# Feed-forward rows as two float32r parts, with the scale on VectorE

## The chip, the cores and the metric

The kernel runs on one core of a Trainium2 chip. The engines of the core are TensorE (PE, matmuls; its weight loads are shown apart as PEld), VectorE (DVE), ScalarE (ACT), GpSimd (POOL) and SyncE (SP, which issues most DMAs). Each works through its own queue in order, and they wait for each other through semaphores. The metric is the device time of one execution in microseconds (us).

## The reference

Four sequences of 2048 tokens with 512 features go through one layer: attention with 16 heads of 32 features, a residual and a layer norm, then a feed-forward layer whose weights are only the signs of the given matrix, a residual and a layer norm again.

```python
q, k, v = (heads(x @ W.T) for W in (Wq, Wk, Wv))
attn = softmax(einsum('nhqd,nhkd->nhqk', q, k) / sqrt(32), axis=3)
x = layernorm(x + einsum('nhql,nhld->nhqd', attn, v))      # heads joined to 512
w = (weights >= 0) * 2 - 1                                  # plain signs, 512 x 512
y = clip(einsum('bsi,oi->bso', x, w) * scale + bias, -100, 100)
x = layernorm(x + y)
```

`scale` and `bias` have one value for each of the 512 outputs. Everything is float32.

## The kernel before

The work is cut into 16 units `n`: four batches of four head groups, each of four heads. A unit has four query blocks `qb` of 512 queries, and a query block has 16 steps, one for each 128 keys. So there are 64 steps in a unit and 1024 in all. The text below calls 16 steps a block and 64 steps a group.

A step does the following, whatever else it carries. `scores` puts the negated row maximum (a bf16 matmul, line 300) and the products of keys and queries (line 306) into four PSUM banks, one for each head, and ScalarE takes the exponentials into a tile `p` (line 313; four buffers of it). `max_unit` computes the scores of a later step a first time (line 248) and VectorE reduces three of the four banks to row maxima (line 255); the fourth is first copied to `moved` by ScalarE (line 267). Every second step, `weighted` multiplies two tiles `p` with the values (line 324), and VectorE adds the result to `oT` (line 336). `add_up` lets POOL add the tiles `p` of a block into `acc` (line 344), for the softmax denominators: 14 additions a block, one for each step but the first and the last.

The other work is spread over the steps as small pieces by a planner (`plan`). Pieces of kind "small" are transpositions, pieces of kind "big" are the projections to K, Q and V (line 206) and the feed-forward (`ffn`, line 532), at most two of the big ones in an odd step, chosen by due time and by a quota for each group. The planner also keeps a rough clock of PE, ACT and DVE (`runs`, `spend`, `give`), by which `take` picks the PSUM bank out of eight that should be free first. The program's order on each engine is fixed when it is built.

The part around the change is the class `Finish`, for one block of 512 tokens whose attention is complete: `load`, `stats`, `rstd` (its power runs on POOL, line 490), `shift` and `norm` make the first layer norm; `turn` transposes a row tile of 128 tokens into PSUM (line 518) and ScalarE copies it to SBUF (line 524); `ffn` multiplies it with the transposed signs `wT["ws"]` (line 532), and VectorE adds the bias (line 537), clips (line 538) and adds the residual (line 540); then comes the second layer norm and the store. For batches 0 to 2 this happens during the steps of the next batch, one row tile per 13 or 11 steps. For the last batch, `finish_last` and `finish_end` squeeze it into the last steps and behind them. The feed-forward of a row tile is cut by columns into thirds of 172, 172 and 168, each a big piece of its own; the last eight row tiles are done whole. There are 64 row tiles in all. The transposed rows lie in `nT` (two buffers), or, for the last batch, in `room`, a larger tile with place for four rows that `make_room` takes from another pool.

The signs are prepared once at the start by POOL (`sign_weights`, lines 147 and 149): the sign and the scale of each output row go into the weight matrix, before it is transposed.

Of the kernel before, what the change touches and what calls it, by code (L numbers as in the profile page):

```python
# [10 lines left out]

F32 = mybir.dt.float32
BF16 = mybir.dt.bfloat16
AF = mybir.ActivationFunctionType
ALU = mybir.AluOpType
AX = mybir.AxisListType
# [4 lines left out]
def kernel(  # L21
# [13 lines left out]
    P = 128  # L35
# [11 lines left out]
    MAX_VAL = 100.0  # L47
    SM_SCALE = 1.0 / math.sqrt(HD)
    STEPS = NQB * NT
    THIRDS = (0, 172, 344, D)  # L50
    W = 2 * P
    LEAD = NT + 6

# [78 lines left out]

    def transpose_weight(name, ic):
        if ic == 0:
            wT[name] = const.tile([P, DC, D], F32, name=f"{name}T")
        i = take()
        pt = cols_of(i, DC, P)
        for oc in range(DC):
            nc.tensor.transpose(pt[:, oc, :], raws[name][:, oc, ts(ic, P)], ident)  # L139
        runs("full", 0.44)  # L140
        nc.scalar.copy(wT[name][:, ic, :].rearrange("p (c o) -> p c o", c=DC), pt)
        give(i, "ACT", 0.6)

    def sign_weights():

        ws = raws["ws"]
        nc.gpsimd.tensor_scalar(ws, ws, 0.0, 2.0, ALU.is_ge, ALU.mult)
        for oc in range(DC):
            nc.gpsimd.tensor_scalar(
                ws[:, oc, :], ws[:, oc, :], 1.0, scale_t[:, oc : oc + 1], ALU.subtract, ALU.mult  # L150
            )

    raws = {n: load_weight(w, n) for n, w in (("wk", wk), ("wq", wq))}
    scale_t = const.tile([P, DC], F32, name="scale_t")
    bias_bc = const.tile([P, D], F32, name="bias_bc")

    def load_rest():
        for n, w in (("wv", wv), ("ws", w_ffn)):
            raws[n] = load_weight(w, n)
        nc.sync.dma_start(out=scale_t, in_=ffn_scale.rearrange("(c p) -> p c", p=P))  # L160
        nc.sync.dma_start(out=bias_bc, in_=ffn_bias.partition_broadcast(P))


# [283 lines left out]
    class Finish:  # L447
# [66 lines left out]
        def turn(self, j):  # L514
            i = take()
            pt = cols_of(i, DC, P)
            for c in range(DC):
                nc.tensor.transpose(pt[:, c, :], self.row(j)[:, ts(c, P)], ident)  # L518
            runs("full", 0.44)
            if self.b < B - 1:  # L520
                self.nT[j] = work.tile([P, DC, P], F32, tag="nT", name="nT")
            else:
                self.nT[j] = self.room[:, j, :].rearrange("p (c q) -> p c q", c=DC)
            nc.scalar.copy(self.nT[j], pt)
            give(i, "ACT", 0.6)

        def ffn(self, j, third):
            cols = slice(0, D) if third is None else slice(THIRDS[third], THIRDS[third + 1])
            i = take()
            py = ps[:, i, : cols.stop - cols.start]  # L530
            for c in range(DC):
                nc.tensor.matmul(  # L532
                    py, lhsT=self.nT[j][:, c, :], rhs=wT["ws"][:, c, cols],
                    start=(c == 0), stop=(c == DC - 1),
                )
            runs("full", 6.8e-3 * (cols.stop - cols.start))
            nc.vector.tensor_tensor(py, py, bias_bc[:, cols], ALU.add)
# [5 lines left out]
        def make_room(self):  # L543

            if self.g < NQB // 2:
                t = kpool.tile([P, S], F32, tag="kT", name="room") if self.g == 0 else shared[0]
                shared[:] = [t]
                self.room = t.rearrange("p (j d) -> p j d", j=NTQ)
            else:
                self.room = xpool.tile([P, NTQ, D], F32, tag="xg", name="room")  # L550

        def store_tile(self, j):
            nc.sync.dma_start(
# [27 lines left out]
    def finish(b, qb, a, every, w, lag):  # L581
        f = Finish(b, qb)
        at(a, f.load)
        for j in range(NTQ):
            at(a + 2 + j, f.stats, 1, j)
        at(a + 6, f.rstd, 1)
        at(a + 7 + lag, f.shift, 1)
        for j in range(NTQ):
            t = a + 8 + lag + every * j
            at(t, f.norm, 1, j)  # L590
            turned = task("small", t + 1, t + 3, f.turn, j)
            for k in range(3):
                task("big", t + 2, t + w, f.ffn, j, k, after=turned)
            at(t + w, f.stats, 2, j)
        e = a + 9 + lag + every * (NTQ - 1) + w
        at(e, f.rstd, 2)
        at(e + 1 + lag, f.shift, 2)
        for j in range(NTQ):
            at(e + 2 + lag + j, f.norm, 2, j)
        at(e + 5 + lag, f.store)  # L600

    def finish_last(qb, last):

        f = Finish(B - 1, qb)
        at(last - 9, f.load_last)
        a = last + 7
        late = qb == NQB - 2
        at(a + 1, f.make_room)
        for j in range(NTQ):
            at(a + j // 2, f.stats, 1, j)  # L610
        at(a + 2, f.rstd, 1)
        at(a + 4, f.shift, 1)
        for j in range(NTQ):
            t = a + 5 + (j if late else 3 * j)
            by = t + 6
            at(t, f.norm, 1, j)
            if late:
                by = total + (-1, 1, 4, 5)[j]
            turned = task("small", t + 1, t + 3, f.turn, j)
            for k in [None] if late else range(3):  # L620
                task("big", by if late else t + 2, by, f.ffn, j, k, after=turned)
            at(by + late, f.stats, 2, j)
        e = total + 7 if late else a + 21
        at(e, f.rstd, 2)
        at(e + 2, f.shift, 2)
        for j in range(NTQ):
            at(e + 3 + j, f.norm, 2, j)
        at(e + 7, f.store)

    def finish_end(qb, last):  # L630

        f = Finish(B - 1, qb)
# [8 lines left out]
        at(total + 3, f.make_room)  # L641
# [223 lines left out]
```

## Time and profile before

| what | value |
|---|---|
| time, median of 3 runs | 4386.38 us (4384.66 to 4386.73) |
| the profiled execution | 4386.25 us |
| its span, first to last instruction | 4384.5 us |
| granted TensorE clock, mean | 0.998 |
| exponentials, ACT, 128x512 | 4096 of 602 ns |
| additions of `p`, POOL, 128x2048 | 889 of about 4.54 us |
| feed-forward matmul lines, PE | 172 or 168 columns, 1344 records (two to a product); 512 columns, 64 records |
| copy of a turned row, ACT | 48 of 641 ns (`nT`), 16 of 608 ns (`room`) |
| bias, clip, residual, DVE | 172 columns: 337, 346, 332 ns; 512 columns: 696, 700, 687 ns |

In the groups of instructions, "mean ns of one" is the time from an instruction's start to its end; matmuls overlap in PE's pipeline, so the spacing of their starts tells more. Idle time is put down to what ended it. The chain of waits follows the last instruction back to what released each step. A table of stretches gives the busy time of each engine between two times, and the timeline shows merged runs of instructions with their start, length and number.

### The profile page before, as it was taken

To read this page: it belongs to the slowest core of one execution; us is meant where nothing else is said; L and a number is where in the kernel's file an instruction comes from. 1 tells how busy PE (TensorE), PEld (TensorE's weight loads), DVE (VectorE), ACT (ScalarE), POOL (GpSimd) and SP (SyncE) were. 2 spreads that over 40 slices of the span, in tenths; PEclk is the share of its full clock that TensorE was granted. 3 is DMA by queue.
4 is the path that set the end of the run, shared out by engine and by line. 5 is a ranking of instruction groups with operands and counts; after the bars stand their busy time and mean duration, and the time that the engine had idled before them with its cause. 6 is when DMAs were issued, how large, how long until landed. Compare 5 with 4: busy or idle time off the path is not lost.

```text
span 4384.5 us, 89302 instructions
## 1 busy us (share of the span) xinstructions
PE 4345.0 (99%) x36092; PEld 2135.5 (49%) x36092; DVE 3315.9 (76%) x5908; ACT 2999.3 (68%) x6173; POOL 4083.3 (93%) x940
## 2 busy tenths in 40 slices
PE   9999999999999999999999999999999999999998
PEld 5444444444454454455445454455544545455443
DVE  6777777777777777777777777777777777777774
ACT  4666666676667667676676766767667676767665
POOL 3999999999999999999999999999999999999993
PEclk9999999999999999999999999999999999999999
DMA  2000000010001000011000100001100000001101
GB/s 88 11 10 14 11 14 10 12 39 22 21 13 27 13 23 20 11 45 36 21 20 11 33 10 21 23 10 49 25 20 21 20 21 23 20 11 33 24 23 49
DMA packets 263351, 101.41 MB, mean 23 GB/s; under 512 B 169372, under 2 KB 239004, under 8 KB 262936
## 3 DMA queue, kind: packets, MB, share of 16 engines
q1 hardware_dynamic: 257656, 91.50, 8.6%
q8 instruction: 282, 4.62, 0.4%
q10 hardware_dynamic: 5280, 4.19, 0.3%
q14 instruction: 133, 1.09, 0.1%
HBM read 54.26 MB, written 33.02 MB: 20 GB/s over the span
## 4 chain that ended last, share of the span: by engine, by line
PE 91%; POOL 6%; DVE 1%; ACT 1%; issue 1%; DMA 0%; ACTq 0%; POOLq 0%; DVEq 0%
PE ps L324 20%; PE ps L248 19%; PE ps L306 19%; PE ps L206 15%; PE ps L300 8%; POOL acc L344 6%; PE ps L532 5%; PE ps L350 3%; PE ps L391 1%; PE ps L195 1%; PE ps L518 1%; ACT p L313 1%; DVE part L255 1%; DMA xs<-in_L_attn_x_dram 0%; PE ps L139 0%
## 5 line engine op out<-in xcount | busy, mean ns | idle before, releaser
L344 POOL TENSOR_TENSOR acc<-acc,p 128x2048 f32<-128x2048 f32 x825 | 3743.7, 4538 | 102.8 <-ACT p L313 42.6
L313 ACT ACTIVATE p<-ps 128x512 f32<-128x512 f32 x4096 | 2114.8, 602 | 1136.0 <-PE ps L306 1108.2
L255 DVE TENSOR_REDUCE part<-ps 128x1 f32<-128x512 f32 x3072 | 1933.0, 683 | 774.6 <-PE ps L248 774.2
L248 PE MATMUL ps<-kT,qT 32*128 32x512 f32 x8192 | 1114.3, 590 | 0.2 <-DVE xg_last L434 0.2
L306 PE MATMUL ps<-qT,kT 32*128 32x512 f32 x8192 | 1073.3, 591 | 0.0
L324 PE MATMUL ps<-p,vv 128*32 128x512 f32 x8192 | 983.4, 598 | 1.8 <-ACT p L313 1.8
L248 PEld LDWEIGHTS ps<-kT,qT 32*128 32x128 f32 x8192 | 542.8, 184 | 381.0 <-issue 194.5
L255 DVE TENSOR_REDUCE part<-moved 128x1 f32<-128x512 f32 x1024 | 691.9, 676 | 3.3 <-ACT moved L267 3.2
L267 ACT COPY moved<-ps 128x512 f32<-128x512 f32 x1024 | 631.0, 616 | 22.1 <-PE ps L248 18.0
L324 PEld LDWEIGHTS ps<-p,vv 128*32 128x32 f32 x8192 | 220.2, 109 | 686.9 <-issue 345.9
L300 PE MATMUL ps<-negm,ones_bf 32*128 32x512 bf16 x4096 | 443.1, 384 | 4.9 <-ACT p L313 2.9
L306 PEld LDWEIGHTS ps<-qT,kT 32*128 32x128 f32 x8192 | 405.8, 184 | 44.3 <-issue 27.5
L336 DVE TENSOR_TENSOR oT<-ps,oT 128x512 f32<-128x512 f32 x448 | 309.7, 691 | 97.4 <-PE ps L324 59.2
L344 POOL TENSOR_TENSOR acc<-p 128x2048 f32<-128x2048 f32 x64 | 290.8, 4544 | 96.0 <-ACT p L313 95.8
L300 PEld LDWEIGHTS <-ones_bf 32*128 32x128 bf16 x4096 | 105.6, 91 | 551.0 <-issue 522.3
L206 PEld LDWEIGHTS ps<-wvT,xT 128*128 128x128 f32 x2048 | 250.9, 191 | 80.3 <-ACT p L313 75.6
L206 PE MATMUL ps<-wvT,xT 128*128 128x128 f32 x2048 | 279.2, 280 | 0.3 <-ACT p L313 0.2
L206 PE MATMUL ps<-xT,wqT 128*128 128x256 f32 x1024 | 248.8, 386 | 2.7 <-ACT p L313 2.7
L206 PE MATMUL ps<-xT,wkT 128*128 128x256 f32 x1024 | 248.7, 387 | 0.0
L206 PEld LDWEIGHTS ps<-xT,wkT 128*128 128x128 f32 x1024 | 184.9, 190 | 68.8 <-ACT p L313 47.0
L206 PEld LDWEIGHTS ps<-xT,wqT 128*128 128x128 f32 x1024 | 184.5, 190 | 66.6 <-ACT p L313 44.9
L532 PEld LDWEIGHTS ps<-wsT,nT 128*128 128x128 f32 x1152 | 167.8, 189 | 94.2 <-ACT p L313 93.3
(75 smaller groups left out, 1722.4 us busy)
## 6 DMA issues: line engine op xcount, KB each, us to landing
xs<-in_L_attn_x_dram SPq DMA_DIRECT2D x64, 256.0 KB
xc<-in_L_attn_x_dram SPq DMA_DIRECT2D x60, 256.0 KB
res<-xc SPq DMA_DIRECT2D x60, 256.0 KB
xg<-res SPq DMA_DIRECT2D x12, 1024.0 KB
out_dram<-xg SPq DMA_DIRECT2D x12, 1024.0 KB
xg_last<-res SPq DMA_DIRECT2D x4, 768.0 KB
out_dram<-xg_last SPq DMA_DIRECT2D x3, 1024.0 KB
raw_wk<-in_L_attn_Wk_dram ACTq DMA_DIRECT2D x4, 256.0 KB
```

What stands on the lines that cost most here:

```text
L206: nc.tensor.matmul(pp, lhsT=lhs(c), rhs=rhs(c), start=(c == 0), stop=(c == DC - 1))
L248: nc.tensor.matmul(ps[:, banks[h], :], lhsT=qT[n, qb][rows, ts(qc, P)], rhs=kT[n][rows, ts(kb, QB)], start=True, stop=True,)
L255: nc.vector.tensor_reduce(part[:, qc, h : h + 1, kb], src, AX.X, ALU.max, negate=True)
L267: nc.scalar.copy(moved, ps[:, banks[-1], :])
L300: nc.tensor.matmul(ps[:, banks[h], :], lhsT=ones_bf[rows, :], rhs=negm[n, qb][rows, :], start=True, stop=False,)
L306: nc.tensor.matmul(ps[:, banks[h], :], lhsT=kT[n][rows, ts(kc, P)], rhs=qT[n, qb][rows, :], start=False, stop=True,)
L313: nc.scalar.activation(p[:, h, :], ps[:, banks[h], :], AF.Exp, scale=SM_SCALE)
L324: nc.tensor.matmul(pb[cols, :], lhsT=vv[n][:, kc, cols], rhs=p[:, h, :], start=(i == 0), stop=(i == 1),)
L336: nc.vector.tensor_tensor(outs[n, qb], pb, outs[n, qb], ALU.add)
L344: nc.gpsimd.tensor_tensor(a, before if kc == 1 else a, p, ALU.add)
L350: nc.tensor.matmul(ps[h * HD : (h + 1) * HD, b, :], lhsT=ones, rhs=p[:, h, :], start=start, stop=stop,)
L532: nc.tensor.matmul(py, lhsT=self.nT[j][:, c, :], rhs=wT["ws"][:, c, cols], start=(c == 0), stop=(c == DC - 1),)
```

## The change

Five things change together.

- `turn` makes two parts of a transposed row tile in place of one copy. ScalarE writes `high` as float32r, which keeps twelve significant bits, and VectorE subtracts it from the row in PSUM and writes the rest as `low`, float32r too. Both have two buffers, for all batches; `room` and `make_room` are gone.
- The transposed signs are a float32r tile, plain -1 and 1. POOL no longer multiplies the scale into them: its second operation is one instruction over all columns in place of four.
- `ffn` multiplies both parts with the signs, eight products into one bank in place of four.
- The scale is loaded as a row of 512 copied to all partitions (`scale_bc`), and VectorE multiplies each result by it, ahead of the bias.
- A row tile's feed-forward is cut into two halves of 256 columns in place of three thirds. The last eight row tiles are still done whole. The planner's clock gets new numbers for the pieces.

```diff
     def transpose_weight(name, ic):
         if ic == 0:
-            wT[name] = const.tile([P, DC, D], F32, name=f"{name}T")
+            kind = F32R if name == "ws" else F32
+            wT[name] = const.tile([P, DC, D], kind, name=f"{name}T")
...
         nc.gpsimd.tensor_scalar(ws, ws, 0.0, 2.0, ALU.is_ge, ALU.mult)
-        for oc in range(DC):
-            nc.gpsimd.tensor_scalar(
-                ws[:, oc, :], ws[:, oc, :], 1.0, scale_t[:, oc : oc + 1], ALU.subtract, ALU.mult
-            )
+        nc.gpsimd.tensor_scalar(ws, ws, 1.0, 0.0, ALU.subtract, ALU.add)
...
-        nc.sync.dma_start(out=scale_t, in_=ffn_scale.rearrange("(c p) -> p c", p=P))
+        nc.sync.dma_start(out=scale_bc, in_=ffn_scale.partition_broadcast(P))
...
             runs("full", 0.44)
-            if self.b < B - 1:
-                self.nT[j] = work.tile([P, DC, P], F32, tag="nT", name="nT")
-            else:
-                self.nT[j] = self.room[:, j, :].rearrange("p (c q) -> p c q", c=DC)
-            nc.scalar.copy(self.nT[j], pt)
-            give(i, "ACT", 0.6)
+
+            high = work.tile([P, DC, P], F32R, tag="high", name="high")
+            low = work.tile([P, DC, P], F32R, tag="low", name="low")
+            nc.scalar.copy(high, pt)
+            spend("ACT", 0.6, clock["PE"] + 0.2)
+            nc.vector.tensor_tensor(low, pt, high, ALU.subtract)
+            give(i, "DVE", 0.7)
+            self.nT[j] = high, low
 
-        def ffn(self, j, third):
-            cols = slice(0, D) if third is None else slice(THIRDS[third], THIRDS[third + 1])
+        def ffn(self, j, half):
+            cols = slice(0, D) if half is None else ts(half, HALF)
+            wide = D if half is None else HALF
             i = take()
-            py = ps[:, i, : cols.stop - cols.start]
-            for c in range(DC):
-                nc.tensor.matmul(
-                    py, lhsT=self.nT[j][:, c, :], rhs=wT["ws"][:, c, cols],
-                    start=(c == 0), stop=(c == DC - 1),
-                )
-            runs("full", 6.8e-3 * (cols.stop - cols.start))
+            py = ps[:, i, :wide]
+            for k, part in enumerate(self.nT[j]):
+                for c in range(DC):
+                    nc.tensor.matmul(
+                        py, lhsT=part[:, c, :], rhs=wT["ws"][:, c, cols],
+                        start=(k == c == 0), stop=(k == 1 and c == DC - 1),
+                    )
+            runs("full", 3.4e-3 * wide)
+            nc.vector.tensor_tensor(py, py, scale_bc[:, cols], ALU.mult)
             nc.vector.tensor_tensor(py, py, bias_bc[:, cols], ALU.add)
             nc.vector.tensor_scalar(py, py, MAX_VAL, -MAX_VAL, ALU.min, ALU.max)
             dst = self.row(j)[:, cols]
             nc.vector.tensor_tensor(dst, dst, py, ALU.add)
-            give(i, "DVE", 0.5 + 3.1e-3 * (cols.stop - cols.start))
+            give(i, "DVE", 0.6 + 4.2e-3 * wide)
...
-            for k in range(3):
+            for k in range(2):
                 task("big", t + 2, t + w, f.ffn, j, k, after=turned)
...
-            for k in [None] if late else range(3):
+            for k in [None] if late else range(2):
                 task("big", by if late else t + 2, by, f.ffn, j, k, after=turned)
```

More of the change, by code (lines that the diff above doesn't have):

```diff
@@ L13 @@
 BF16 = mybir.dt.bfloat16
+F32R = mybir.dt.float32r
 AF = mybir.ActivationFunctionType
@@ L49 @@
     STEPS = NQB * NT
-    THIRDS = (0, 172, 344, D)
+    HALF = D // 2
     W = 2 * P
@@ L147, in sign_weights @@
         nc.gpsimd.tensor_scalar(ws, ws, 0.0, 2.0, ALU.is_ge, ALU.mult)
-        for oc in range(DC):
-            nc.gpsimd.tensor_scalar(
-                ws[:, oc, :], ws[:, oc, :], 1.0, scale_t[:, oc : oc + 1], ALU.subtract, ALU.mult
-            )
+        nc.gpsimd.tensor_scalar(ws, ws, 1.0, 0.0, ALU.subtract, ALU.add)
     raws = {n: load_weight(w, n) for n, w in (("wk", wk), ("wq", wq))}
-    scale_t = const.tile([P, DC], F32, name="scale_t")
+    scale_bc = const.tile([P, D], F32, name="scale_bc")
     bias_bc = const.tile([P, D], F32, name="bias_bc")
@@ L540, in ffn @@
             nc.vector.tensor_tensor(dst, dst, py, ALU.add)
-            give(i, "DVE", 0.5 + 3.1e-3 * (cols.stop - cols.start))
[L543 to L550, printed above, removed]
+            give(i, "DVE", 0.6 + 4.2e-3 * wide)
         def store_tile(self, j):
@@ L607, in finish_last @@
         late = qb == NQB - 2
-        at(a + 1, f.make_room)
         for j in range(NTQ):
@@ L640, in finish_end @@
                 at(total + 3, f.norm, 1, j - 1)
-        at(total + 3, f.make_room)
         for j in range(NTQ):
```

## The prediction

> **What bounds the kernel now.** I read the page's busy times and chain first, because they name the engine. Its span, 4384.5 us, belongs to a profiled execution of 4386.25 us (1.75 us outside the span); the median of the runs shown is 4386.38 us, so sums made against this execution carry over.
>
> ```profile
> span 4384.5 us, 89302 instructions
> ...
> PE 4345.0 (99%) x36092; PEld 2135.5 (49%) x36092; DVE 3315.9 (76%) x5908; ACT 2999.3 (68%) x6173; POOL 4083.3 (93%) x940
> ...
> PE 91%; POOL 6%; DVE 1%; ACT 1%; issue 1%; DMA 0%; ACTq 0%; POOLq 0%; DVEq 0%
> ```
>
> Here the reader is to see that TensorE (PE) looks saturated and holds nine tenths of the chain, and that POOL is busy 93% too. A busy share does not say which of two nearly full engines paces a stage, so I next cut the span into groups: 64 steps, four query blocks of 16 steps, cut where POOL starts a block's first addition.
>
> ```profile
> core 0: us, PE busy (x) PEld busy (x) DVE busy (x) ACT busy (x) POOL busy (x), PEclk, DMA share, GB/s
> 545.89:803.89 258.00, 253.85 (x2136) 117.77 (x2132) 191.06 (x320) 173.83 (x356) 253.93 (x58) 1.00 0.06 12
> 868.39:1127.08 258.69, 257.97 (x2196) 123.81 (x2192) 190.86 (x320) 181.66 (x372) 253.94 (x57) 1.00 0.13 32
> 1127.08:1391.36 264.28, 263.73 (x2224) 130.31 (x2220) 206.69 (x371) 180.64 (x370) 256.05 (x59) 1.00 0.07 16
> 1391.36:1656.99 265.63, 265.47 (x2241) 131.15 (x2240) 207.50 (x373) 184.78 (x380) 256.01 (x59) 1.00 0.08 19
> 1656.99:1922.56 265.57, 265.42 (x2241) 131.09 (x2240) 207.37 (x373) 184.78 (x380) 256.00 (x59) 1.00 0.08 19
> 1922.56:2195.69 273.13, 272.98 (x2309) 137.20 (x2312) 207.84 (x374) 192.40 (x398) 256.13 (x59) 1.00 0.13 34
> ...
> 4071.75:4278.18 206.43, 200.92 (x1575) 94.89 (x1573) 154.02 (x302) 140.93 (x288) 194.24 (x46) 0.99 0.10 25
> 4278.18:4384.46 106.28, 90.64 (x574) 41.07 (x573) 51.40 (x109) 60.45 (x133) 39.17 (x18) 0.92 0.15 50
> ```
>
> Columns: stretch, its length, then busy time of PE, PEld, DVE, ACT, POOL. A group of batch 0 takes 258.0 to 258.7 us, one of batches 1 and 2 mostly 265.5 to 265.8 (the first, 1127 to 1391, 264.3), the fourth of these batches 273.1 and 272.9, those of batch 3 267.9, 269.1, 269.3. POOL's own timeline tells why.
>
> ```profile
> 545.89 4.57 POOL L344 TENSOR_TENSOR acc<-p 128x2048 f32<-128x2048 f32 x1
> 550.54 59.89 POOL L344 TENSOR_TENSOR acc<-acc,p 128x2048 f32<-128x2048 f32 x13
> 610.38 4.56 POOL L344 TENSOR_TENSOR acc<-p 128x2048 f32<-128x2048 f32 x1
> ...
> 1523.35 4.54 POOL L344 TENSOR_TENSOR acc<-p 128x2048 f32<-128x2048 f32 x1 [1.39 <-ACT p L313]
> ```
>
> In batch 0 the 14 additions of a block run without a gap: 610.38 - 545.89 = 64.49 us, 4.606 us per addition, and the next block begins at once: POOL sets the pace. Batch 0 has no feed-forward. From batch 1 on POOL waits for ScalarE's exponentials at the start of most blocks (1.39 us here), and PE sets the pace. So POOL's floor is 56 x 4.606 = 257.9 us a group, and 259.9 with the two powers of `rstd` (1.0 us each) of a finish. Only 5.7 us a group lie between the present time and that floor: this is the limit on what less PE work can give.
>
> **The change, part by part.** *Feed-forward on PE.* How PE's pieces are priced shows in its timeline of one odd step:
>
> ```profile
> 1531.82 1.41 PE L532 MATMUL ps<-wsT,nT 128*128 128x168 f32 x8
> 1533.07 1.05 PE L206 MATMUL ps<-wvT,xT 128*128 128x128 f32 x8
> 1534.05 0.40 PE L300 MATMUL ps<-negm,ones_bf 32*128 32x512 bf16 x4
> 1534.28 1.03 PE L306 MATMUL ps<-qT,kT 32*128 32x512 f32 x8
> ```
>
> A third of 168 columns holds PE from 1531.82 to 1533.07, 1.25 us, of which four float32 products of 168 columns are 1.12 and the change of array shape the rest. A V piece (four products of 128) takes 0.98, 0.85 without the change of shape. Four bf16 products of 512 columns, side by side in the array, take 0.23. So float32 costs 1.67 ns a column and bf16 0.42 to 0.45. Before, a row tile costs 512 x 4 x 1.67 = 3.41 us; the chain has three thirds in a row at 3.48. After, it is 16 products of 256 columns. No float32r product is in the trace. Its bounds: the bf16 row (0.107 us for 256 columns) and the float32 row: in the chain one K or Q piece of four 256-column products takes 1.93 us and two in a row 3.65, so 1.72 a piece, 0.43 a product. I take the bf16 end: each float32 product appears as two recorded matmuls (the K pieces' 512 products are the 1024 records below), each at two bf16 prices, and an operand cut to twelve bits against a plain sign leaves no second part to multiply. That is an inference, so the other end stays as a rival. A half is then 0.85 us, a tile 1.71, and PE gains 1.70 us a tile.
>
> ```profile
> L206 PE MATMUL ps<-xT,wkT 128*128 128x256 f32 x1024 | 248.7, 387 | 0.0
> ...
> L537 DVE TENSOR_TENSOR ps<-ps,bias_bc 128x172 f32<-128x172 f32 x112 | 37.7, 337 | 14.6 <-PE ps L532 14.3
> ```
>
> The new products have one weight load of 128x128 for 0.107 us of matmul. In the V piece above, eight full-size loads and eight matmuls of 0.107 end within 0.98 us: loads of this size and type hide at this rate. If they hid less, the nearest row is a transposition's load, 140 ns: half 1.12 us, tile 2.24, gain 1.17. I take 0.107 and keep 0.14 for the range.
>
> The Trainium skill speaks against this change here: "TensorE: Matmul & The Clock Gate", Part 3, The mechanism, says that a weight load overlaps matmuls in flight only when their row groups differ, and all loads here fill all rows. Its section LDWEIGHTS gives 128/1.2 = 107 ns a load, so by that rule a half is an estimated 8 x 0.214 = 1.71 us, a tile 3.42, and the gain zero. The V piece would then need 1.71 us and takes 0.98, so the measurement decides.
>
> *VectorE.* An operation of 172 columns takes 337 ns (last line above), of 512 columns 696: 1.06 ns a column, so 426 ns for 256. A tile had 9 x 0.337 = 3.05 us and gets 8 x 0.426 + 0.69 (the subtraction that makes the low part) = 4.10; with whole rows, 3 x 0.70 become 5 x 0.70. Sum: 56 x 1.05 + 8 x 1.4 = 70 us. Bounds: nothing, or all 70 on the path (no gain: it is more work on the same engine). I take nothing: DVE is idle 58 us of a 265.6 us group and gets 4.2 more. If that cover went, row maxima would free banks late and PE's next `max_unit` would wait.
>
> *The new wait.* The subtraction waits for ScalarE's copy of the high part; behind it on DVE stand the feed-forward operations, the oT addition and the row maximum of `moved`.
>
> ```profile
> 1550.00 0.64 ACT L524 COPY nT<-ps 128x512 f32<-128x512 f32 x1
> 1550.21 0.68 DVE L255 TENSOR_REDUCE part<-moved 128x1 f32<-128x512 f32 x1
> ...
> 1552.82 1.89 DVE L255 TENSOR_REDUCE part<-ps 128x1 f32<-128x512 f32 x3 [1.93 <-PE ps L248]
> ```
>
> The copy ends at 1550.64. The subtraction would end at about 1551.35, the row maximum after it at 1552.05, and DVE's next work is released only at 1552.82. Cover 0.8 us; where it is gone, PE loses at most that, 48 times, 38 us.
>
> *Edits with one answer.* POOL's four scaling instructions (7.9 us) become one of about 7.1 us, in an idle stretch that ends with the first addition at 92.47. The scale's DMA on SP becomes a broadcast, ahead of the bias, and is wanted first after 1127 us. ScalarE's copy stays (0.64 us). All three cost nothing.
>
> *Where it lands.* In the order of PE's instructions, thirds become halves per group so: 12 to 8 in batches 1 and 2; 12 to 8, 14 to 10, 15 to 10, and 20 to 13 in the last three full blocks. At 1.147 and 0.853 us PE gains 6.9, 7.5, 8.7 and 11.9 us.
> - First three groups of batches 1 and 2: 265.6 - 6.9 = 258.7, under POOL's 259.9. Two nearly full engines lose a little to each other: 868 to 1127 took 258.7 on a floor of 257.9. I add 1.0: 260.9. Gain 3.4 + 4.7 + 4.7 + 4.6 + 4.9 + 4.8 = 27.1.
> - Fourth groups: still PE-bound, 6.9 less 0.4 of such losses, twice: 13.0.
> - Batch 3: 267.9 to 262.0, 269.1 to 262.6, 269.3 to 261.6: 5.9 + 6.5 + 7.7. Last three blocks: PE 206.4 - 11.9 = 194.5, POOL 42 x 4.606 + 4 = 197.4; I say 199: 7.4. Together 27.5.
> - Tail, 4278 to 4384: up to 4342 PE is the chain and gains 3 x 1.7 + 2 x 1.7 = 8.5. Then DVE is: five operations a row instead of three (3.5 + 0.87 of statistics, against PE's present 3.44 a row), and with two buffers for the parts in place of `room`, the third row's copy waits for the first row's products. I charge 5.5. Gain 3, bounds -5 and +9.
>
> Sum 70.6 us: 4386.3 - 70.6 = 4316.
>
> **The rivals.**
> 1. *Loads or DVE not fully hidden.* Loads at 0.14: gain 1.17 a tile, group 260.9 + 0.8, so 6 x 3.7 + 2 x 4.4 + 22 = 53 and no gain in the tail: 4333. A quarter of DVE's 70 us on the path as well: 4350. For it: both prices are extrapolated. Against it: the V piece, DVE's idle 58 us.
> 2. *The change doesn't do what it says: two passes, or loads in series.* A half then costs 1.71 and a tile what it costs now; DVE's extra is hidden: 4386, at most 4400 with the tail. For it: no float32r row. Against it: as above.
> 3. *Slower: float32r runs at the float32 rate.* 16 x 0.43 = 6.88 us a tile, 3.45 more, on PE, which paces all groups with feed-forward: 64 x 3.45 = 221, less about 10 in blocks that POOL holds now: 4597. It decides from 0.213 us per 256-column product. For it: operands are four bytes wide, as in the row that costs 0.43.
>
> **How the numbers follow.** Forecast 0.75 (own range 4298 to 4332: all friction gone and a good tail gain another 18; twice the friction and a bad tail cost 16), rival 1 0.13, rival 2 0.06, rival 3 0.06. The range runs from 4298, below which POOL's floor leaves little, to 4348, where rival 1 nearly ends; 0.8 lie in it. About 0.2% (8.8 us) is what this kernel's measurement can tell from no change: faster 0.87; same 0.04, most of rival 2; slower 0.09, rival 3 and the tail of 2.
>
> **What would show it.** Right: the two matmul lines of `ffn` start 0.11 us apart, a half 0.85 us before PE's next piece; 256-column DVE operations near 426 ns; POOL's additions gapless over blocks of batches 1 and 2, groups near 261 and 266; POOL's share of the chain well over 6%; DVE near 3385 us busy. Wrong: groups still 265 with POOL waiting (products or loads slower), POOL's additions longer than 4.54 us, PE waiting on DVE's row maxima, or a tail over 106 us.

## The result and the profile after

The changed kernel takes 4395.44 us in the median (4392.38 to 4396.86), the kernel before beside it on the same chip 4386.03 us (4383.17 to 4387.36): a ratio of 1.0021 with an interval of 1.0013 to 1.0029. It is slower by some 9 us, where 70 us of gain were forecast. The profiled execution took 4393.68 us, with a span of 4391.9.

The page of the changed kernel, its busy times and the chain by engine:

```profile
span 4391.9 us, 88393 instructions
...
PE 4338.6 (99%) x35644; PEld 2083.5 (47%) x35644; DVE 3382.1 (77%) x5924; ACT 2995.1 (68%) x6173; POOL 4082.7 (93%) x937
...
PE 88%; POOL 7%; DVE 2%; ACT 1%; issue 1%; DMA 0%; ACTq 0%; SPq 0%; POOLq 0%; DVEq 0%
```

DVE works 66 us more (70 were forecast). PE is busy for only 6 us less, although it issues cheaper matmuls. The same stretches as before, cut again at POOL's first addition of a block, with the columns in the same order:

```profile
867.08:1125.73 258.65, 257.94 (x2196) 123.78 (x2192) 190.93 (x320) 181.66 (x372) 253.89 (x57) 1.00 0.12 32
1125.73:1391.01 265.28, 264.73 (x2190) 126.51 (x2187) 210.45 (x371) 179.98 (x370) 256.11 (x59) 1.00 0.07 15
1391.01:1658.12 267.11, 267.11 (x2210) 127.45 (x2209) 211.33 (x373) 184.30 (x381) 256.05 (x60) 1.00 0.08 19
1658.12:1925.14 267.02, 267.02 (x2210) 127.57 (x2209) 211.35 (x373) 184.31 (x381) 256.09 (x60) 1.00 0.08 19
1925.14:2198.02 272.88, 272.66 (x2284) 134.75 (x2286) 212.43 (x374) 192.63 (x398) 256.09 (x60) 1.00 0.13 34
4078.80:4286.37 207.57, 200.81 (x1523) 87.96 (x1521) 160.86 (x303) 141.10 (x288) 194.44 (x47) 0.98 0.10 25
4286.37:4391.80 105.43, 76.14 (x540) 37.84 (x536) 63.13 (x122) 60.43 (x133) 39.25 (x18) 0.86 0.15 51
```

Batch 0, which has no feed-forward, is unchanged (258.65 against 258.69). The groups of batch 1 take 265.3, 267.1, 267.0 and 272.9 us, where 260.9 and 266.6 were forecast. Against before, the first addition comes 1.15 us earlier (91.32 against 92.47), batch 0 takes 0.2 less, batches 1, 2 and 3 (this one up to its last block) take 3.7, 3.4 and 2.45 more, and the tail 0.8 less: together 7.4 us, the difference of the two spans. The granted clock is 1.00 in all these groups, before and after; it is lower only in the last 313 us.

Where the saved matmul time went is seen on PE's lines (line, engine, operands, count, busy us, mean ns of one; line 247 is `max_unit`, 535 the feed-forward):

```profile
L247 PE MATMUL ps<-kT,qT 32*128 32x512 f32 x8192 | 1194.0, 592 | 2.2 <-ACT p L312 1.8 <-DVE xg_last L544 0.4
...
L535 PE MATMUL ps<-wsT,high 128*128 128x256 f32 x448 | 83.3, 309 | 0.0
L535 PE MATMUL ps<-wsT,low 128*128 128x256 f32 x448 | 72.7, 285 | 0.0
```

The row of `max_unit` in the kernel before:

```profile
L248 PE MATMUL ps<-kT,qT 32*128 32x512 f32 x8192 | 1114.3, 590 | 0.2 <-DVE xg_last L434 0.2
```

All matmuls of the feed-forward's line taken together, overlaps counted once, keep PE busy for 154.8 us, against 264.6 before: 110 us less. But `max_unit`, whose 8192 records the change does not touch, went from 1114.3 us to 1194.0: 80 us more. One record of it is as long as before (592 ns, before 590), so the records only overlap less: they start further apart, and the growth is no work. The timeline of one odd step shows what it is:

```profile
1454.76 0.74 PE L535 MATMUL ps<-wsT,high 128*128 128x256 f32 x4
1454.85 1.89 DVE L254 TENSOR_REDUCE part<-ps 128x1 f32<-128x512 f32 x3 [0.67 <-PE ps L247]
...
1455.33 0.64 PE L535 MATMUL ps<-wsT,low 128*128 128x256 f32 x4
...
1455.82 1.06 PE L205 MATMUL ps<-wvT,xT 128*128 128x128 f32 x8
...
1456.66 0.42 DVE L540 TENSOR_TENSOR ps<-ps,scale_bc 128x256 f32<-128x256 f32 x1
...
1457.03 1.02 PE L305 MATMUL ps<-qT,kT 32*128 32x512 f32 x8
1457.11 0.43 DVE L541 TENSOR_TENSOR ps<-ps,bias_bc 128x256 f32<-128x256 f32 x1
...
1457.58 0.43 DVE L542 TENSOR_SCALAR ps<-ps 128x256 f32<-128x256 f32 x1
1457.89 1.82 PE L247 MATMUL ps<-kT,qT 32*128 32x512 f32 x8
...
1458.12 0.42 DVE L544 TENSOR_TENSOR xg<-xg,ps 128x256 f32<-128x256 f32 x1
...
1458.59 0.29 PEld L247 LDWEIGHTS ps<-kT,qT 32*128 32x128 f32 x2 [0.51 <-DVE xg L544]
```

The half takes PE from 1454.76 to 1455.82, 1.06 us, and everything behind it moves up. On DVE the half's four operations begin only when the three row maxima are done, at 1456.66, and end at 1458.54, 0.65 us after `max_unit` begins. The half's PSUM bank is held until then. PE comes to `max_unit` at 1457.89, and its last two weight loads stand until 1458.59 for that bank: the eight matmuls take 1.82 us in place of 1.03. The kernel before, in the step whose PE lines the prediction shows:

```profile
1531.92 1.89 DVE L255 TENSOR_REDUCE part<-ps 128x1 f32<-128x512 f32 x3 [0.65 <-PE ps L248]
...
1533.73 0.33 DVE L537 TENSOR_TENSOR ps<-ps,bias_bc 128x168 f32<-128x168 f32 x1
...
1534.09 0.34 DVE L538 TENSOR_SCALAR ps<-ps 128x168 f32<-128x168 f32 x1
...
1534.46 0.33 DVE L540 TENSOR_TENSOR xg<-xg,ps 128x168 f32<-128x168 f32 x1
...
1535.14 1.03 PE L248 MATMUL ps<-kT,qT 32*128 32x512 f32 x8
```

Here the third's last DVE operation ends at 1534.79 and `max_unit` begins at 1535.14: 0.35 us are to spare. The table of waits has the same over the whole run, first for the kernel before, then for the changed one (waiting line, releaser, us in total, times, longest; L524 is the subtraction):

```profile
PEld ps L248 <- DVE xg L540: 6.9, 23, 0.5
```

```profile
DVE low L524 <- ACT high L522: 43.1, 60, 6.2
...
PEld ps L247 <- DVE xg L544: 27.8, 62, 0.5
...
PEld ps L247 <- DVE low L524: 7.8, 24, 0.5
```

The wait of the loads shows only part of it: 0.51 us in the step above, where the eight matmuls take 0.79 us more. What `max_unit` costs is told better by the time from its first matmul to the first matmul of the next piece, sorted by what the step carries. Worked out so from the starts of the matmuls between 1130 and 4070 us:

| `max_unit` after | before | after |
|---|---|---|
| a third or half and a V piece | 0.97 us (100 times) | 1.69 us (62) |
| a third or half alone | 1.64 (6) | 1.98 (12) |
| a half and a K or Q piece | 0.96 (6) | 0.96 (8) |
| a turned row and a V piece | 0.98 (9) | 1.54 (20) |

(Some expectations below have 1.40 us and 28 times in the last row. That count takes in eight steps with a transposition of incoming rows beside the V piece, which the change does not touch: 1.05 us, before 1.03.)

Two waits, then: one after halves, of 0.72 us, 62 times (45 us), and one after turned rows, of 0.56, 20 times (11 us). The second looks like this in the timeline; the bank is the one that the row was turned into, and DVE gives it back with the subtraction:

```profile
1551.18 0.69 DVE L524 TENSOR_TENSOR low<-ps,high 128x512 fp32r<-128x512 f32 x1 [0.38 <-ACT high L522]
1551.43 1.63 PE L247 MATMUL ps<-kT,qT 32*128 32x512 f32 x8
...
1551.93 0.30 PEld L247 LDWEIGHTS ps<-kT,qT 32*128 32x128 f32 x4 [0.31 <-DVE low L524]
```

From the first addition of batch 1 to that of the last group, the time from each piece's start to the next piece's adds up so: the feed-forward takes 74 us less, `max_unit` 71 more, the other pieces 12 more. That is the 8 us by which this stretch grew. Of the 71, 56 are the two waits, and 7 belong to halves that stand alone in a step. A half beside a K or Q piece, which holds PE for 1.9 us in place of 1.0, does not wait.

### The profile page after: what moved, and what is told of

It is laid out like the page before. It is cut to its first block, busy times and chain, and to the rows that moved or that the text cites. A ratio compares the mean times of both kernels' runs of the same rounds, so it can differ in the third digit from the quotient of the medians.

```text
span 4391.9 us, 88393 instructions
## 1 busy us (share of the span) xinstructions
PE 4338.6 (99%) x35644; PEld 2083.5 (47%) x35644; DVE 3382.1 (77%) x5924; ACT 2995.1 (68%) x6173; POOL 4082.7 (93%) x937
## 3 DMA queue, kind: packets, MB, share of 16 engines
q14 instruction: 133, 1.09, 0.1%
## 4 chain that ended last, share of the span: by engine, by line
PE 88%; POOL 7%; DVE 2%; ACT 1%; issue 1%; DMA 0%; ACTq 0%; SPq 0%; POOLq 0%; DVEq 0%
PE ps L247 20%; PE ps L323 19%; PE ps L305 18%; PE ps L205 15%; PE ps L299 8%; POOL acc L343 7%; PE ps L535 3%; PE ps L349 3%; ACT p L312 1%; DVE part L254 1%; PE ps L390 1%; PE ps L194 1%; PE ps L517 1%; DVE st L481 0%; DMA xs<-in_L_attn_x_dram 0%
## 5 line engine op out<-in xcount | busy, mean ns | idle before, releaser
L247 PE MATMUL ps<-kT,qT 32*128 32x512 f32 x8192 | 1194.0, 592 | 2.2 <-ACT p L312 1.8
L305 PE MATMUL ps<-qT,kT 32*128 32x512 f32 x8192 | 1084.7, 594 | 0.0
L247 PEld LDWEIGHTS ps<-kT,qT 32*128 32x128 f32 x8192 | 569.9, 184 | 431.5 <-issue 210.5
L299 PE MATMUL ps<-negm,ones_bf 32*128 32x512 bf16 x4096 | 459.1, 384 | 6.6 <-ACT p L312 3.5
L299 PEld LDWEIGHTS <-ones_bf 32*128 32x128 bf16 x4096 | 106.2, 91 | 553.0 <-issue 520.6
L333 DVE COPY oT<-ps 128x512 f32<-128x512 f32 x64 | 44.3, 692 | 131.0 <-PE ps L323 129.1
```

Source lines behind the costliest of these rows:

```text
L247: nc.tensor.matmul(ps[:, banks[h], :], lhsT=qT[n, qb][rows, ts(qc, P)], rhs=kT[n][rows, ts(kb, QB)], start=True, stop=True,)
L299: nc.tensor.matmul(ps[:, banks[h], :], lhsT=ones_bf[rows, :], rhs=negm[n, qb][rows, :], start=True, stop=False,)
L305: nc.tensor.matmul(ps[:, banks[h], :], lhsT=kT[n][rows, ts(kc, P)], rhs=qT[n, qb][rows, :], start=False, stop=True,)
```

## The experiments

The kernel before ran beside each of these; its median was 4385.85 to 4386.03 us, so that their times may be compared with each other. Four theories are told apart. In the expectations, A says that DVE holds the half's bank until after its burst of operations, and that PE waits for it in the steps where it gets there sooner. B says that PE's own work sets the time (float32r or its loads slower than they look). C says that DVE's work as a whole sets the pace of these steps, and D that the subtraction and its wait do.

**No scale operation.** A burst of three operations instead of four; the result lacks the scale.

```diff
-            nc.vector.tensor_tensor(py, py, scale_bc[:, cols], ALU.mult)
```

> The changed kernel without the multiplication by the scale (so the output lacks the scale). Theory A: each half's PSUM bank is held by VectorE's four operations (1.88 us in the trace), all eight banks are wanted again by the next max_unit, and PE waits about 0.8 us a half, which eats the 0.9 us a half that float32r saves. With three operations (1.41 us) the wait falls by 0.47 us: groups of batches 1 and 2 from 267.1 to about 263.3 us, total near 4395 - 55 = 4340 us. Rival B, PE's own work (its new products, weight loads, switches) is the bound: groups stay at 267, total 4390 to 4396.

Measured: 4353.96 us (4351.68 to 4355.87), ratio to the kernel before 0.9927 (0.9912 to 0.9941). The operation taken out is 52.9 us of DVE's busy time (47.4 + 5.5); the kernel becomes 41.5 us faster, though DVE was idle for 1010 us. In the timeline of this run the step is (same columns):

```profile
1458.00 0.42 DVE L543 TENSOR_TENSOR xg<-xg,ps 128x256 f32<-128x256 f32 x1
1458.22 1.37 PE L247 MATMUL ps<-kT,qT 32*128 32x512 f32 x8
```

The residual ends 0.20 us after `max_unit` begins, where it was 0.65 us, and `max_unit` takes 1.37 us in place of 1.82. After a half and a V piece it takes 1.22 us in the mean (62 times) in place of 1.69. The time is 14 us over what A expected and some 36 under B's 4390: B falls, and part of the wait stays.

**High part only.** Four products of a half instead of eight; DVE and ACT as in the changed kernel.

```diff
-            for k, part in enumerate(self.nT[j]):
+            for k, part in enumerate(self.nT[j][:1]):
...
```

> The changed kernel without the four products of the low part in each piece (so the result has only the high part's twelve bits); VectorE's work is unchanged. PE gets 0.48 us less a half. Theory A: PE only comes earlier to the bank that VectorE still holds, groups stay within 0.7 us of 267.1, total 4385 to 4395 (some gain in the tail). Rival B, PE is the bound: 8 x 0.48 = 3.8 us less a group, 112 halves and 8 whole rows make about 60 us, total near 4335.

Measured: 4392.35 us (4389.48 to 4394.55), ratio 1.0014 (1.0004 to 1.0023): half the feed-forward's matmuls are worth 3 us. The matmul lines and the waits of this run:

```profile
L247 PE MATMUL ps<-kT,qT 32*128 32x512 f32 x8192 | 1224.9, 592 | 8.9 <-ACT p L312 2.3 <-DVE xg L544 0.5 <-DVE xg_last L544 0.4
...
L535 PE MATMUL ps<-wsT,high 128*128 128x256 f32 (+1 forms) x480 | 92.0, 318 | 4.3 <-ACT high L522 4.3
```

```profile
PEld ps L247 <- DVE xg L544: 61.3, 70, 1.2
```

`max_unit` grows again, to 1224.9 us, and after a half and a V piece it now takes 2.17 us. So PE's work no longer sets these steps: the 0.48 us taken from a half are given back one piece later (2.17 - 1.69).

**The bank freed early.** The scale operation writes into SBUF, and the rest of the burst works there, so that the bank is free after the first operation.

```diff
-            nc.vector.tensor_tensor(py, py, scale_bc[:, cols], ALU.mult)
-            nc.vector.tensor_tensor(py, py, bias_bc[:, cols], ALU.add)
-            nc.vector.tensor_scalar(py, py, MAX_VAL, -MAX_VAL, ALU.min, ALU.max)
+            y = work.tile([P, D], F32, tag="y", name="y")[:, :wide]
+            nc.vector.tensor_tensor(y, py, scale_bc[:, cols], ALU.mult)
...
+            nc.vector.tensor_tensor(y, y, bias_bc[:, cols], ALU.add)
+            nc.vector.tensor_scalar(y, y, MAX_VAL, -MAX_VAL, ALU.min, ALU.max)
...
-            nc.vector.tensor_tensor(dst, dst, py, ALU.add)
...
+            nc.vector.tensor_tensor(dst, dst, y, ALU.add)
...
```

> The changed kernel, but the multiplication by the scale writes to an SBUF tile, and bias, clip and residual work there: VectorE has the same four operations, the bank is free after the first (0.43 us). Theory A (the held bank): PE's wait goes, the max_unit matmul line falls from 75.1 to about 68 us busy a group, groups near 261, total near 4325. Rival C (VectorE's throughput in these steps, whichever bank): the row maxima come as late as before, groups stay near 267, total about 4395. If operations with both operands in SBUF beside POOL's additions get slower, VectorE's or POOL's means show it, and the time may rise.

Measured: 5097.31 us (5092.84 to 5099.66), ratio 1.162 (1.1603 to 1.1638). The time says nothing on A against C, because the operations themselves changed. Their groups in this run:

```profile
L544 DVE TENSOR_SCALAR y<-y 128x256 f32<-128x256 f32 x112 | 339.1, 3028 | 3.8
L543 DVE TENSOR_TENSOR y<-y,bias_bc 128x256 f32<-128x256 f32 x112 | 305.8, 2730 | 3.8
L546 DVE TENSOR_TENSOR xg<-xg,y 128x256 f32<-128x256 f32 x96 | 231.5, 2412 | 3.4
L541 DVE TENSOR_TENSOR y<-ps,scale_bc 128x256 f32<-128x256 f32 x112 | 46.7, 417 | 5.9 <-PE ps L535 5.5
```

With one operand in PSUM an operation takes 417 ns. With all operands in SBUF it takes 2.4 to 3.0 us, as the last section tells. The single steps do tell the bank from DVE's pace:

```profile
1422.28 0.42 DVE L541 TENSOR_TENSOR y<-ps,scale_bc 128x256 f32<-128x256 f32 x1
...
1423.50 1.02 PE L247 MATMUL ps<-kT,qT 32*128 32x512 f32 x8
...
1424.41 4.51 DVE L544 TENSOR_SCALAR y<-y 128x256 f32<-128x256 f32 x1
...
1428.95 4.67 DVE L546 TENSOR_TENSOR xg<-xg,y 128x256 f32<-128x256 f32 x1
...
1434.86 0.61 PE L299 MATMUL ps<-negm,ones_bf 32*128 32x512 bf16 x2 [8.16 <-DVE part L254]
```

The operation that reads the bank ends 0.80 us before `max_unit` begins. The burst ends 10 us after `max_unit` has begun, and still `max_unit` takes only its 1.02 us. So it is in 60 of 61 steps with a half and a V piece between 1130 and 4670 us: 0.96 us to the next piece, though the burst always ends later than `max_unit` begins. What `max_unit` waits for in the changed kernel is the bank and not the end of DVE's work. DVE's work is waited for later, at the row maxima (L299). What an early bank would be worth with a burst of normal length stays open.

**The scale operation alone, on the kernel before.** Plain signs, the scale on DVE, but float32 and thirds.

```diff
...
             runs("full", 6.8e-3 * (cols.stop - cols.start))
+            nc.vector.tensor_tensor(py, py, scale_bc[:, cols], ALU.mult)
             nc.vector.tensor_tensor(py, py, bias_bc[:, cols], ALU.add)
...
```

> The kernel before, with plain signs and the scale as a fourth VectorE operation on each third; float32, thirds and one copy stay. VectorE's burst a third goes from 1.08 to 1.45 us. Theory A: in the timeline of before, VectorE was done 0.35 us ahead of the next max_unit, so 0.37 us more costs next to nothing: 4386 to 4400 us. Rival C' (any VectorE work lands on the path): 168 x 0.37 + 8 x 0.7 = 68 us, total near 4454.

Measured: 4415.31 us (4414.06 to 4416.91), ratio 1.0067 (1.0052 to 1.0082), 29 us slower, in between what the theories had expected. DVE gets 62 us of work; `max_unit` after a third and a V piece goes from 0.97 to 1.14 us (99 times), after a third alone from 1.64 to 1.96. So the kernel before had hardly room for one more operation in these steps, less than the 0.35 us of the one step that I had read, and A's "next to nothing" was wrong here.

**Thirds.** The changed kernel with 172, 172 and 168 columns again.

```diff
-            cols = slice(0, D) if half is None else ts(half, HALF)
-            wide = D if half is None else HALF
+            cols = slice(0, D) if half is None else slice(THIRDS[half], THIRDS[half + 1])
+            wide = cols.stop - cols.start
...
```

> The changed kernel with the columns cut into 172, 172 and 168 again, everything else as changed (float32r parts, scale on VectorE). VectorE's burst a piece falls from 1.88 to about 1.45 us. Theory A (the bank is held too long in one step) with products that cost about 0.12 us at any width: little wait is left, groups near 262 to 263, total 4335 to 4365. If float32r products under 256 columns run at the float32 rate (0.28 us for 172 columns), a third costs PE 2.3 us in place of 1.2, groups near 279, total near 4560. Rival B (PE's work is the bound): 12 x 1.05 in place of 8 x 1.05 us a group, total near 4440.

Measured: 4412.90 us (4410.20 to 4415.20), ratio 1.0060 (1.0043 to 1.0077): a miss. The timeline of a third in this run:

```profile
1456.72 0.68 PE L535 MATMUL ps<-wsT,high 128*128 128x172 f32 x4
...
1457.24 0.61 PE L535 MATMUL ps<-wsT,low 128*128 128x172 f32 x4
...
1457.69 1.08 PE L205 MATMUL ps<-wvT,xT 128*128 128x128 f32 x8
```

Eight products of 172 columns take 0.97 us, against 1.06 with 256 columns. That rules out a price in proportion to the columns: a product of 172 columns costs nearly as much as one of 256. So PE reaches `max_unit` only a little sooner than with a half, the burst of four shorter operations is 1.5 us instead of 1.9, and `max_unit` waits 0.43 us instead of 0.72, but 99 times instead of 62. Both sizes lose about the same to waits, and thirds have 12 pieces a group to pay for instead of 8.

**Halves beside K and Q.** If a long piece on PE covers the burst, the planner can provide one: it pairs a half with a K or Q piece first, and only then with a V piece.

```diff
                     elif k == 1:
-                        can = values[:1] or thirds[:1] or wide[:1]
+                        can = values[:1] or wide[:1] or thirds[:1]
+                    elif thirds and wide:
+                        can = thirds[:1] + wide[:1]
                     elif thirds and values:
```

> The changed kernel; the planner alone is changed: it lets a half of the feed-forward share its step with a K or Q piece (1.72 us of PE) before a V piece (0.85). By the order of PE's instructions 42 halves then share a step with a K or Q piece (9 before), 32 with V (68 before). PE's total work is the same. Theory A: with 0.87 us more PE work in the step, VectorE is done before the next max_unit and the wait of about 0.8 us goes for some 33 to 36 halves: total near 4395 - 28 = 4367. Rival B: same work, same time, 4390 to 4400.

Measured: 4374.20 us (4373.07 to 4375.16), ratio 0.9973 (0.9963 to 0.9984). This version leaves nothing out and beats both kernels, the changed one by 21 us. The timeline of a step in this run:

```profile
1455.22 1.89 PE L205 MATMUL ps<-xT,wqT 128*128 128x256 f32 x8
...
1457.53 0.42 DVE L544 TENSOR_TENSOR xg<-xg,ps 128x256 f32<-128x256 f32 x1
...
1458.13 1.03 PE L247 MATMUL ps<-kT,qT 32*128 32x512 f32 x8
```

The burst is unchanged and ends 0.18 us ahead of `max_unit`, which takes its 1.03 us. Of the halves, 37 now stand beside K or Q and cost 0.98 us in `max_unit`; the 29 that stay beside a V piece still cost 1.70. Same instructions, same engines, another order, and DVE just as busy (3383.0 us, 3382.1 in the changed kernel): B and C, by which the time would have stayed, fall, and A holds.

**No subtraction.** High part only as above, and the low part not made at all; the bank is given back after ACT's copy, and the planner's clock is told so.

```diff
-            low = work.tile([P, DC, P], F32R, tag="low", name="low")
             nc.scalar.copy(high, pt)
-            nc.vector.tensor_tensor(low, pt, high, ALU.subtract)
...
```

> As the run with the high part alone, and without the subtraction that makes the low part (so VectorE has 64 x 0.69 = 44 us less and doesn't wait for ScalarE's copy; the result has twelve bits of the rows). Its difference to that run (4392) is the price of the subtraction and its wait. Prediction's step (it is covered, nothing): 4385 to 4393, a few us of it in the tail. Rival D (the new wait, 43 us of VectorE's idle time, lands on the path): 4335 to 4350.

Measured: 4367.91 us (4367.27 to 4369.18), ratio 0.9960 (0.9945 to 0.9975), against 4392.35 with the subtraction. So the subtraction and its wait cost 24 us, between the two expectations. `max_unit` after a turned row and a V piece goes back from 1.54 to 0.99 us (20 times, 11 us). Cut by POOL's first additions, 8 us of the difference of the two profiled executions lie in batches 1 and 2, and 14 in the last group and behind it, where the rows of the last batch are finished; these were not traced to steps. D holds, as a second cause beside A, with about half of what it expected.

**Two parts of the weights.** The scale goes back into the signs, which are then split into two float32r parts, so that a half has twelve products and DVE only three operations; one staging buffer is given up for the room.

```diff
...
-            for k, part in enumerate(self.nT[j]):
+            for k, (part, w) in enumerate(((high, "ws"), (high, "rest"), (low, "ws"))):
...
-            nc.vector.tensor_tensor(py, py, scale_bc[:, cols], ALU.mult)
...
```

> A full version: the scale goes back into the weights on POOL, the scaled signs are split into two float32r parts as the rows are, and a half is twelve products (high x main, high x rest, low x main) in place of eight; no scale on VectorE, three operations a half. (The buffers of incoming x go from three to two, for room.) PE has about 0.48 us more a half than the changed kernel, VectorE 0.47 us less. Theory A: the burst of 1.41 us ends before the next max_unit, since PE's part of the step is longer; group 265.6 - 17.1 + 8 x 1.55 = 260.9, against POOL's floor of 259.9, so about 261.5; total 4335 to 4350. Rival B (PE's work is the bound): 60 us more than the run without the scale, total near 4415.

Measured: 4387.67 us (4385.17 to 4389.56), ratio 1.0003 (0.9994 to 1.0013): a miss. The wait after a half and a V piece is gone (0.96 us, 62 times), but the half takes 1.53 us on PE, which costs as much as the wait did. A turned row and a V piece still wait (1.55, 20 times), and the first addition comes at 99.33 us, 8 us later than in the changed kernel, with one staging buffer less.

**Long steps for all halves and turned rows.** In the middle of the kernel a half gets a K, a Q or two V pieces, and so does a turned row.

```diff
...
+                    long = wide[:1] or values[:2]
+                    if middle and any(map(on_vector, must)):
+                        can = long
...
+                    elif middle and thirds and not turns:
+                        can = thirds[:1] + long
+                    elif middle and turns:
+                        can = long
...
```

> The changed kernel with only the planner changed, further than before: a step that has a half of the feed-forward also gets a K or Q piece or two V pieces, whenever there is one (by PE's order 40 halves share with a K or Q piece and 34 with two V pieces; 8 stay with one V piece; before 9, 0 and 68), and so does a step in which a row tile is turned. Theory A: after these steps the max_unit matmuls take 0.96 us in place of 1.69 (half and one V) and 1.40 (turn and one V); 62 x 0.73 and about 15 x 0.4 us of the changed kernel go in batches 1 to 3: total near 4395 - 50 = 4345. Rival B (PE's total work): unchanged work, 4390 to 4400. If the longer steps starve POOL or ScalarE, less: 4360 to 4375.

Measured: 4378.71 us (4376.92 to 4382.99), ratio 0.9985 (0.9977 to 0.9994): faster than before, but not than the simple pairing, and far from what was expected. `max_unit` takes 0.96 us after a half with a K or Q piece (34) and with two V pieces (30). After a turned row the wait is gone too (0.96 us, 42 times beside a K or Q piece). But 32 odd steps are left empty, and there `max_unit` takes 1.48 us in place of 0.96, and the piece with the negated maximum (L299) ahead of it 1.15 in place of 0.23: together 46 us, more than the 33 that are missing to the expected gain.

**The same planner on the kernel before.**

> The kernel before with this same planner (thirds, float32, scale in the weights). It has almost no such waits (0.97 us after a third and a V piece), so theory A expects nothing from the planner: 4380 to 4395. If the planner's smoothing were the gain in itself, it would show here too: 4340 to 4360.

Measured: 4450.05 us (4447.62 to 4450.63), ratio 1.0146 (1.0130 to 1.0161). Neither expectation was met. This planner alone costs the kernel before 64 us, so under it the change is worth 4450.05 - 4378.71 = 71 us. That is the size that was forecast, but it is no proof of the forecast: this planner was written for halves, and 12 thirds fit into its long steps worse than 8 halves (33 thirds are left alone in a step, at 1.64 us). It does show that what the change is worth depends on the order of the pieces.

**Two parts of the weights, long steps.** The last two ideas together.

> The version with split weights (twelve products a half, three VectorE operations, two buffers for x) with this planner. Its steps with a half and a V piece had no wait left (0.96 us), only halves alone (1.64 us, 13 of them) and turns with a V piece (1.40, 28): theory A expects 4388 - 15 = 4373, so less than the planner gives the changed kernel.

Measured: 4419.68 us (4418.49 to 4421.06), ratio 1.0078 (1.0064 to 1.0092): a miss. After halves nothing waits any more (0.96 us), the 31 empty odd steps still do (1.46), and the halves, at 1.53 us, now make the longest steps longer still. Against the long steps alone the feed-forward takes 44 us more and `max_unit` 9 less from batch 1 to the last group, and the first addition comes 7 us later. These come to 42 us, and the two runs differ by 41.

## Why the prediction was wrong

*Feed-forward on PE: right.* A product of 256 columns appears as one record and takes 0.12 us, near the bf16 end of the bounds (0.107) and far from 0.43. A half takes 1.06 us with its change of array shape, 1.25 was a third. A tile goes from 3.75 to 2.12 us, a gain of 1.63 where 1.70 was forecast. Between 1130 and 4070 us PE spends 74 us less in the feed-forward. Loads are hidden: eight loads and eight products end within 1.06 us. The Trainium skill says ("TensorE: Matmul & The Clock Gate", Part 3, The mechanism) that a load overlaps matmuls in flight only when the row groups differ, though the section speaks of a background weight buffer too; read as loads in series, with the 107 ns a load that the page's section LDWEIGHTS gives, a half would be an estimated 1.71 us, and this trace does not agree. Rivals 2 and 3 are out.

*VectorE: the step that failed.* The size was right (426 ns forecast for 256 columns, 420 to 433 measured; 70 us forecast, where 9 x 0.337 is 3.03 and not 3.05, which would make it 71; 66 measured). Wrong was "I take nothing: DVE is idle 58 us of a 265.6 us group and gets 4.2 more". The idle time of a group says nothing of the one step where the work falls. The step whose PE lines I quoted had the answer in its DVE lines, which I did not use: DVE begins the third's operations at 1533.73, after the row maxima. Four operations of 0.426 us with the gaps of 0.03 between them end at 1535.52, while PE, which begins the piece at 1531.82, would with 0.85 for the half, 0.98 for V and 1.09 for the scores be at `max_unit` at 1534.74. So the burst ends 0.8 us after PE gets there, in every half beside a V piece. In the changed kernel's step it was 0.65 us, and such steps lose 0.72 us in the mean. The mechanism stood in the prediction, as a clause on row maxima that free banks late; the bank that was late was the feed-forward's own, and the clause was given no price. PE's gain made it worse: the faster half is what brought PE to the bank ahead of DVE. Rival 1 had the right engine, but as a quarter of DVE's extra, with 4350 as its end.

*The new wait: wrong too.* It was costed at nothing, with 0.8 us of cover and 38 us as its bound. It costs 24 us. That this lies inside the bound is in part luck: the bound counted the 48 rows of batches 0 to 2, and some 14 us were lost in the last group and behind it, mostly on rows that it left out. The cover was read in one step, at 1550 us, where a K piece of 1.94 us runs on PE; in the changed kernel 20 turned rows stand beside a V piece, where 0.56 us a time are lost, and beside K or Q `max_unit` takes its 0.96 us.

*The sum.* The scale operation costs 41.5 us and the subtraction 24.4, each measured by its removal. Taken together, which assumes that the two add up, they are 66 us: 4395 - 66 = 4329 lies in the forecast's own range of 4298 to 4332. So the gain on PE was there, and the two terms took it back. They were costed at nothing up to the tail; some 13 of the 66 us lie in the tail (it goes from 105.5 to 99.1 us without the scale operation, and from 104.2 to 97.5 without the subtraction), for which the forecast had charged 5.5. The 13 us between 4329 and the forecast of 4316 were not traced.

*POOL's floor, the start, the tail.* POOL's additions stayed at 4.54 us and batch 0 at its floor. That the first addition comes 1.15 us earlier shows nothing: in other runs with the same start it comes at 92.8 to 94.9 us. The tail gained 0.8 us instead of 3, inside its bounds. POOL's share of the chain went from 6% to 7%, where well over 6% had been named as the sign of success: groups never came down to POOL's floor.

*The signs.* Groups still at 265 and PE waiting on DVE's row maxima had both been named as what would make the prediction wrong. Groups at 265 came, but had been put down to slow products or loads, which was not the cause. PE did wait on DVE, but for the residual that frees the half's bank and for the subtraction, and not for the row maxima.

## What to carry to other kernels

Cover is a matter of the step in which work falls, not of an engine's idle share: take the one step with the new work, write down when each engine reaches the shared buffer, and move both engines by the change. An engine made faster arrives earlier at whatever it shares, so a gain on it and an extra on its partner must be costed in one sum. And a busy TensorE row can hold waits: where a matmul line grows that nobody changed, look for the bank that it stands for.

## What the runs showed of the hardware

- A float32r product of 256 columns appears as one record, and four of them take 0.49 us to the next piece (the `low` products of the timelines above), 0.12 each, against two records and 0.43 us for float32. With 172 columns four take 0.45 us, 0.11 each: a third fewer columns gained almost nothing.
- In the run with the bank freed early, operations of DVE with all operands in SBUF take 2.4 to 3.0 us in the mean for 256 columns beside POOL's additions, which keep their 4.54 us; with one operand in PSUM 0.42 us. Of these operations 211 last over 1 us, and every one of them ends 0.15 to 0.29 us after an addition of POOL has ended; those of 256 columns that meet no addition take 0.29 to 0.43 us. In the tail of that run, where POOL's additions are over, the same lines are short, even though they are twice as wide:

```profile
L543 DVE TENSOR_TENSOR y<-y,bias_bc 128x512 f32<-128x512 f32 x8 | 5.5, 692 | 0.3
...
L544 DVE TENSOR_SCALAR y<-y 128x512 f32<-128x512 f32 x8 | 3.4, 426 | 0.3
```

  The Trainium skill agrees ("SBUF — State Buffer", Who interferes with whom): an operation of VectorE with two SBUF inputs, or in a mode that uses both ports, cannot run beside a GpSimd operation that reads SBUF, and the one that comes second stands until the other is done. The ends just behind POOL's additions agree with that. So a burst that works in PSUM is worth holding a bank for in this kernel.
